# A graph layer with a convolution by points: columns of a bin side by side, and one transpose for the distance factors of m

## The chip, the cores and the metric

The kernel runs on one core of a Trainium2 chip. TensorE multiplies matrices and writes PSUM; VectorE (DVE in the profile), ScalarE (ACT) and GpSimd (POOL) work on elements; SyncE (SP) and POOL issue most of the DMAs. The metric is device time in microseconds from the first to the last instruction of one execution; the median of three executions stands for the kernel. The profiled execution is a further one, with a time of its own.

## What is computed

For 64 graphs of 256 nodes with 256 channels (all float32), after a layer norm and a ReLU that give `h`:

```
xc     = transpose(h)                                      # channels, nodes
c      = relu(bn1(conv1(xc)))                              # 1 tap
x_conv = relu(bn2(conv2(c)) + xc)                          # 17 taps
s      = h @ w_se.T + b_se                                 # 3 numbers a node
dist   = |s_n|^2 + |s_m|^2 - 2 s_n.s_m
A      = exp(-dist) * adj
x_nmp  = A @ relu(h @ w_msg.T + b_msg)
out    = x + GRU([x_conv, x_nmp], h)                       # gates r, z, n
```

The GRU's products are the largest part: 768 inputs and outputs of gates by 256 nodes for each graph, from three sources (`h`, `x_nmp`, `x_conv`).

## The kernel before

**Tiling.** Two graphs (`G`) make an item `i`, a tile of 512 columns; there are 32 items. Four items make a batch `b` of eight graphs (`GB`), and the main loop (line 1000) runs over eight batches. In a batch the second convolution is done for all eight graphs; the other parts are done item by item.

**The second convolution.** It is computed by evaluating polynomials at points. The 256 nodes of a graph are 16 residues by 16 blocks (`NW`). `split_steps(j)` (line 691) takes item j's output `h1` of the first convolution and writes differences to `V` and sums to `U`; `fft.odd` and `fft.even` turn these into 16 bins of (mostly) complex values, with `T`, `Sv` and `PT` as further tiles. `products(b, m)` (line 744) then multiplies, for each bin, three operands by three 256x256 weight matrices, on TensorE: the moving operand of one product is one bin of one half of the channels, 8 graphs by 16 blocks, 128 columns. The results go to `Yv` and `Yu`, and `branch_back`, `odd_back`, `q_back`, `p_back` and `join(j)` lead back to nodes; `join(j)` ends with `residual` for item j (lines 786 to 789: L788 on VectorE, L789 on ScalarE), and gives that item's `x_conv`.

All these tiles are seen through `Slots` (line 28): partition, then graph and half of the channels (16), then real or imaginary, then slot n, then 16 blocks. One bin's columns for one half of the channels so lie in 8 pieces of 16, `v[:, k::DC, 0, :]` at line 757. `Yu` is `V` itself: when the products no longer need `V`, the results are written over it, in the same layout, so that `split_steps(j)` of the next batch overwrites just what `join(j)` has read.

**Distances.** `message(i)` (line 792) computes messages and the three numbers `s`, and fills `Z`: block 0 with factors of n (for each of four chunks of nodes -2s, s^2, 1), and blocks 1 and 2 with factors of m (s, 1, s^2) for the two chunks of m, each repeated for the four rows of chunks. `embed(i)` (line 815) transposes the three blocks and copies them to `ZT` at once. `affinity(i)` (line 822) makes four small products of `ZT` with itself, an exponential of each on ScalarE (L830), and a product with `adj` on VectorE (L836).

**Gates.** `gates(i, dc)` (line 865) starts the products with `h` and `x_nmp`, calls `early` after those of r, calls `wait` before the products with `x_conv`, and ends with tanh on ScalarE (L889 `tr`, L896 `nn`, L905 `tz`) and VectorE's parts (L891 to L913). Its PSUM tiles come from a ring of five, `acc`; another ring of three is `aux`.

**Order.** It is written out by hand: every engine works through its instructions in the order in which the program issues them. For VectorE a planner, `Pace` (line 236), keeps a queue of small steps (splits, transforms, joins, statistics). It estimates TensorE's and VectorE's times while the program is written, and issues steps from the queue where VectorE is expected to be free; `flush(mark)` issues all up to a mark. So the order of `pace.add` is VectorE's order among these steps. The part of the loop that the change touches is in lines 1048 to 1094: after the products, the last backward steps end with the mark `scaled`, then follow `join(0)`, statistics of another item and `join(1)`; in the gates of the batch's first item `wait` flushes `scaled`, issues `affinity(i + 2)` and the first convolution of the next batch's first item (`conv1(nxt)`), queues `split_steps(nxt)`, then `join(2)`. `join(3)` is queued after the second gates and `conv1(nxt + 1)`.

Of the kernel before, what the change touches and what calls it, by code (L numbers as in the profile page):

```python
# [13 lines left out]
FP = mybir.dt.float32  # L14
U16 = mybir.dt.uint16
AF = mybir.ActivationFunctionType
# [11 lines left out]
class Slots:  # L28

    def __init__(self, t, A, n, E):
        self.t = t.rearrange("p (a c n e) -> p a c n e", a=A, c=2, n=n)

    def __call__(self, c, s, n=1, step=1):
        if c is None:
            v = self.t.rearrange("p a c n e -> p (a c) n e")
        else:
            v = self.t[:, :, c]
        return v[:, :, s:s + step * (n - 1) + 1:step, :]  # L40
# [261 lines left out]
def kernel(  # L302
# [26 lines left out]
    nc = tc.nc  # L329
    P = 128  # L330
    B, N, D = x.shape
    G = 2
    GB = 8
    PB = GB // G
    NB = B // GB
    DC = D // P
    MC = N // P
    W = G * N
    TAPS = c2_wT.shape[1]
    SE = se_wT.shape[1]  # L340
    KD = 3 * SE
    Q = 32
    L = 16
    NW = N // L
# [4 lines left out]
    const = ctx.enter_context(tc.tile_pool(name="const", bufs=1))  # L349
# [19 lines left out]
    def chunk(t, g, c):  # L369
        return t[:, g * N + c * P:g * N + (c + 1) * P]  # L370


    X, ADJ, Y = {}, {}, {}
# [62 lines left out]
    Ut, Vt = (const.tile([P, SL], FP, name=n) for n in ("U", "V"))  # L436
    PTt, Svt, Tt = (const.tile([P, SL // 2], FP, name=n) for n in ("PT", "Sv", "T"))
    SPARE = {2: Svt, 3: PTt}
    fft = Fft(nc.vector, nc.scalar)
# [74 lines left out]
    pace = Pace()  # L514

    def mm(p, w, v, columns, **kw):
        nc.tensor.matmul(p, w, v, **kw)  # L517
        pace.tensor(columns)

    def transpose(p, v):  # L520
        nc.tensor.transpose(p, v, ident)  # L521
        pace.tensor(P / 2)

    def aux():
        return psum.tile([P, W], FP, name="aux", bufs=3)

    def acc():
        return psum.tile([P, W], FP, name="acc", bufs=5)
# [76 lines left out]
    s1, h1_shift = fold_bn(bn1, "bn1")  # L605


    Z = const.tile([P, 1 + MC, G * MC, Q], FP, name="z")
    nc.gpsimd.memset(Z, 0.0)
    nc.gpsimd.memset(Z[:, 0, :, 2 * SE:KD], 1.0)  # L610
    nc.gpsimd.memset(Z[:, 1:, :, SE:2 * SE], 1.0)
    ZT = const.tile([P, (1 + MC) * P], FP, name="zT")

    h1 = const.tile([P, G * DC, L, NW + 2], FP, name="h1")
    nc.gpsimd.memset(h1, 0.0)

    U, V = (Slots(t, GB * DC, L // 2, NW) for t in (Ut, Vt))
    PT, Sv, T = (Slots(t, GB * DC, L // 4, NW) for t in (PTt, Svt, Tt))
    Yu = V


    def transpose_h(i):
# [52 lines left out]
    def conv1(i, other=acc):  # L675
        if i >= B // G:
            return
        for o in range(DC):
            p = acc() if o == 0 else other()
            for k in range(DC):  # L680
                mm(p, w_c1[:, k, o * P:(o + 1) * P], HT[i][:, k, :], W, start=(k == 0), stop=(k == DC - 1))
            v = h1.rearrange("p (g o) s b -> p o g s b", o=DC)[:, o, :, :, 1:1 + NW]
            u = p.rearrange("p (g s b) -> p g s b", g=G, b=NW)
            if i == 0:
                nc.vector.tensor_scalar(v, u, s1[:, o:o + 1], h1_shift[:, o:o + 1], ALU.mult, ALU.add)
                nc.vector.tensor_scalar(v, v, 0.0, None, ALU.max)
            else:
                nc.scalar.activation(v, u, AF.Relu, bias=h1_shift[:, o:o + 1], scale=s1[:, o:o + 1])
        pace.vector(0, pace.pe + ACT)

    def split_steps(i):
        if i >= B // G:
            return []
        j = i % PB
        hv = h1.rearrange("p a (c h) b -> p (a c) h b", c=2)
        A = slice(2 * G * j * DC, 2 * G * (j + 1) * DC)
        q = []
        for s, b in ((4, 0), (0, 1)):
            a, bb = hv[:, :, s:s + 4, b:b + NW], hv[:, :, s:s + 4, b + 1:b + 1 + NW]
            q += [fft.sub(V(None, s, 4)[:, A], a, bb), fft.add(U(None, s, 4)[:, A], a, bb)]  # L700
        return q


# [40 lines left out]
    def products(b, m, between=None):  # L744
        p = [acc() for _ in range(3)]
        for n in range(2):
            if n and between:
                between()
            for kind, v in enumerate(operands(2 * m + n)):
                if v is None:  # L750
                    load_kind(b, 2 * m + n + 3, kind)
                    continue
                for o in range(DC):
                    for k in range(DC):
                        mm(p[kind][:, (n * DC + o) * P:(n * DC + o + 1) * P],
                           WB[b, 2 * m + n, kind][:, k, o * P:(o + 1) * P],
                           v[:, k::DC, 0, :], P, start=(k == 0), stop=(k == DC - 1))
                load_kind(b, 2 * m + n + 3, kind)
        p1 = work.tile([P, W], FP, name="p1")
        pv = [t.rearrange("p (n a e) -> p a n e", n=2, e=NW) for t in (p1, p[1], p[2])]  # L760
        if m < 7:
            nc.scalar.copy(p1, p[0])
            if m < 4:
                re, im = Yv(m % 2, m // 2 * 2, 2), Yv(m % 2, 4 + m // 2 * 2, 2)
            elif m < 6:
                re, im = Yu(m - 4, 0, 2), Yu(m - 4, 2, 2)
            else:
                t = Yu.t[:, :, :, 6:8, :].rearrange("p a c n e -> p n a c e")
                re, im = t[:, 0], t[:, 1]
            pace.vector(2 * W, pace.pe + PSUM)  # L770
            nc.vector.tensor_sub(re, pv[0], pv[2])  # L771
            nc.vector.tensor_add(im, pv[0], pv[1])  # L772
        else:
            half = W // 2
            nc.scalar.copy(p1[:, :half], p[0][:, :half])
            nc.scalar.mul(Yu(0, 4)[:, :, 0, :], p[0][:, half:].rearrange("p (a e) -> p a e", e=NW), 0.5)
            nc.scalar.mul(Yu(1, 4)[:, :, 0, :], p[1][:, half:].rearrange("p (a e) -> p a e", e=NW), 0.5)
            pace.vector(W, pace.pe + PSUM)
            nc.vector.tensor_sub(Yu(0, 5)[:, :, 0], pv[0][:, :, 0], pv[2][:, :, 0])
            nc.vector.tensor_add(Yu(1, 5)[:, :, 0], pv[0][:, :, 0], pv[1][:, :, 0])  # L780
# [11 lines left out]
    def message(i):  # L792
        MSG[i] = work.tile([P, G, MC, D + SE], FP, name="msg")
        for g in range(G):
            for c in range(MC):
                p = acc() if g * MC + c == 3 else aux()
                for k in range(DC):
                    mm(p[:, :D + SE], chunk(HT[i][:, k], g, c), w_msg[:, k, :], D + SE,
                       start=(k == 0), stop=(k == DC - 1))
                pace.vector(D, pace.pe + PSUM)  # L800
                nc.vector.tensor_add(MSG[i][:, g, c, :], p[:, :D + SE], b_msg)  # L801
        s = MSG[i][:, :, :, D:]
        flat = s.rearrange("p g c s -> p (g c) s")
        nc.scalar.mul(Z[:, 0, :, :SE], flat, -2.0)
        nc.scalar.activation(Z[:, 0, :, SE:2 * SE], flat, AF.Square)
        for c in range(MC):
            z = Z[:, 1 + c].rearrange("p (g x) s -> p g x s", x=MC)
            for x in range(MC):
                nc.scalar.copy(z[:, :, x, :SE], s[:, :, c])
                nc.scalar.activation(z[:, :, x, 2 * SE:KD], s[:, :, c], AF.Square)  # L810
        for g in range(G):
            nc.scalar.activation(MSG[i][:, g, :, :D], MSG[i][:, g, :, :D], AF.Relu)


    def embed(i):
        p = aux()
        for j in range(1 + MC):
            transpose(p[:, j * P:(j + 1) * P], Z[:, j].rearrange("p q s -> p (q s)"))
        nc.scalar.copy(ZT, p[:, :(1 + MC) * P])


    def affinity(i):
# [116 lines left out]
    odd, even, halved, scaled = (Mark() for _ in range(4))  # L939
# [1 line left out]
    joined = [Mark() for _ in range(PB)]  # L941

    def forward():
        pace.add(fft.odd(V, T, Sv), odd)
        pace.add(fft.even(U, PT, T), even)

    w_ih = const.tile([P, 2 * DC, 3 * D], FP)
    w_hh = const.tile([P, DC, 3 * D], FP)
# [51 lines left out]
    for b in range(NB):  # L1000
        i = b * PB
# [48 lines left out]
        def join(j):  # L1050
            pace.add(fft.join(Yu, Yv, T, slice(2 * G * j, 2 * G * (j + 1))))
            pace.add([(W, lambda o=o: residual(i + j, o)) for o in range(DC)], joined[j])
# [10 lines left out]
        pace.flush(normed[1])  # L1063
        turn_h(nxt + 1)

        def wait():
            pace.flush(scaled)
            affinity(i + 2)
            conv1(nxt, aux)
            pace.add(split_steps(nxt), halved)  # L1070
            join(2)
            pace.flush(joined[0])
        gates(i, 0, wait, lambda i=i: embed(i + 2))
        if b == 0:
            transpose_a(i + 2)
            load_y(0)
# [5 lines left out]
        def early():  # L1082
            join_h(nxt + 1)
            pace.flush(normed[2])
            turn_h(nxt + 2)
        gates(i, 1, None, early)
        pace.flush(halved)
        conv1(nxt + 1)
        join(3)
        pace.add(split_steps(nxt + 1), halved)  # L1090
        pace.add(norm_steps(nxt + 3)[0], normed[3])
        aggregate(i + 2)
# [87 lines left out]
```

## Time and profile before

| | |
|---|---|
| median of three executions | 1830.07 us (1827.06 to 1830.39) |
| profiled execution: time, span | 1830.99 us, 1829.2 us |
| TensorE matmuls | 7494 instructions, busy 98% of the span |
| TensorE weight loads | 7494, 61% |
| VectorE | 2596 instructions, 75% |
| ScalarE | 1444 instructions, 40% |
| GpSimd | 357 instructions, 12% |
| granted TensorE clock | 0.995 |
| HBM | 156.6 MB read, 44.3 MB written, 110 GB/s |

The page gives each engine's busy time, the chain of work that ended last, and groups of instructions (line, engine, operation, output<-inputs, shape, count, then busy time, mean duration in ns, and the engine's idle time before them with what ended it). A timeline row gives a start in us from the span's start, a busy time, and a count of merged instructions. One float32 matmul of the program is two instructions in the trace, and most matmuls stand under L517, the helper that issues them; the vector steps of the convolution stand under L59 to L65, and the scalings under L68, for the same reason. Matmuls overlap in the pipeline, so the distance from one start to the next says more than a duration.

### The profile page before, as it was taken

Reading aid. Unit: us, or ns where it says so; the run is one execution under the profiler, and the core shown is the slowest. Engines: PE = TensorE matmul, PEld = TensorE weight load, DVE = VectorE, ACT = ScalarE, POOL = GpSimd, SP = SyncE. Lnnn points to the kernel's source line nnn. Section 1 sums busy time; section 2 is a strip of 40 time slices with the busy share of each in tenths; the row PEclk is TensorE's granted clock in tenths of the full one; section 3 lists DMA queues with packets and bytes.
Section 4 is the critical chain, followed back from the end, with each engine's and each line's share of the span. In section 5 each row is a group of like instructions: output and inputs, shape, how many; then the busy total and the mean of one; then the engine's idle time right before and its main releaser. Section 6 shows DMA issues by size and latency. Waiting matters only on the chain.

```text
span 1829.2 us, 21881 instructions
## 1 busy us (share of the span) xinstructions
PE 1794.1 (98%) x7494; PEld 1112.1 (61%) x7494; DVE 1367.0 (75%) x2596; ACT 727.6 (40%) x1444; POOL 220.7 (12%) x357
## 2 busy tenths in 40 slices
PE   5999999999999999999999999999999999999998
PEld 3787454964569544784448645595546944487453
DVE  4889669795879849797697967888587984979422
ACT  2525532364323642255422653236432463224321
POOL 2210102101111011111012000110111110111000
PEclk9999999999999999999999999999999999999999
DMA  7777553854538444564347545385544744164011
GB/s 197 242 256 229 114 105 91 244 138 113 108 95 257 104 104 92 156 192 119 85 99 218 163 98 107 87 261 119 115 101 121 222 106 95 41 187 114 8 39 35
DMA packets 250482, 245.96 MB, mean 134 GB/s; under 512 B 142936, under 2 KB 176500, under 8 KB 250371
## 3 DMA queue, kind: packets, MB, share of 16 engines
q1 hardware_dynamic: 216634, 183.83, 36.9%
q0 software_dynamic: 30784, 58.07, 13.9%
q10 hardware_dynamic: 2953, 2.66, 0.7%
q8 instruction: 59, 0.97, 0.2%
q14 instruction: 52, 0.43, 0.1%
HBM read 156.56 MB, written 44.30 MB: 110 GB/s over the span
## 4 chain that ended last, share of the span: by engine, by line
PE 93%; DMA 3%; DVE 2%; ACT 1%; issue 0%; SPq 0%; ACTq 0%; DVEq 0%
PE acc L517 80%; PE aux L517 10%; PE aux L521 2%; DMA taps<-in_c_wT_dram 2%; PE aux L829 1%; DMA filt<-fo 1%; DVE Yv L59 1%; DMA wb<-filt 0%; DVE T L65 0%; DVE Yv L62 0%; DVE msg L801 0%; ACT fo L716 0%; DVE st L559 0%; DVE Yv L771 0%; DVE V L772 0%
## 5 line engine op out<-in xcount | busy, mean ns | idle before, releaser
L517 PE MATMUL acc<-xnm,w_ih 128*128 128x512 f32 x768 | 353.1, 592 | 0.0
L517 PE MATMUL acc<-hT,w_hh 128*128 128x512 f32 x768 | 350.5, 592 | 0.0
L517 PE MATMUL acc<-Yv,w_ih 128*128 128x512 f32 x768 | 342.7, 596 | 1.9 <-ACT Yv L789 1.9
L517 PEld LDWEIGHTS acc<-Yv,w_ih 128*128 128x128 f32 x768 | 145.8, 191 | 185.4 <-issue 182.8
L517 PEld LDWEIGHTS acc<-xnm,w_ih 128*128 128x128 f32 x768 | 144.7, 190 | 176.0 <-issue 174.1
L517 PEld LDWEIGHTS acc<-hT,w_hh 128*128 128x128 f32 x768 | 143.9, 190 | 164.6 <-issue 154.3
L891 DVE SCALAR_TENSOR_TENSOR gn<-tr,gn 128x512 f32<-128x512 f32 x64 | 44.2, 690 | 200.2 <-ACT tr L889 200.1
L889 ACT ACTIVATE tr<-acc,b_rz 128x512 f32<-128x512 f32 x64 | 44.0, 687 | 354.6 <-PE acc L517 354.6
L925 POOL DMA_DIRECT2D out_dram<-y x62 | 38.2, 620 | 789.1 <-DVE y L924 763.9
L517 PE MATMUL acc<-V,wb 128*128 128x128 f32 x1024 | 124.8, 275 | 0.0
L517 PE MATMUL acc<-U,wb 128*128 128x128 f32 x1024 | 124.3, 276 | 0.0
L517 PEld LDWEIGHTS acc<-U,wb 128*128 128x128 f32 x1024 | 120.4, 192 | 3.5 <-DVE T L59 2.0
L59 DVE SCALAR_TENSOR_TENSOR V<-T,V 128x256 f32<-128x256 f32 (+2 forms) x224 | 121.8, 612 | 0.3
L517 PEld LDWEIGHTS acc<-V,wb 128*128 128x128 f32 x1024 | 119.5, 192 | 0.0
L517 PE MATMUL acc<-hT,w_c 128*128 128x512 f32 x228 | 106.5, 608 | 1.7 <-ACT hT L633 1.3
L517 PE MATMUL aux<-e,msg 128*128 128x256 f32 x464 | 104.9, 379 | 0.0
L517 PEld LDWEIGHTS aux<-e,msg 128*128 128x128 f32 x464 | 87.1, 190 | 17.7 <-issue 6.9
L565 POOL TENSOR_TENSOR rstd<-rstd,neg_half 128x4 f32<-128x4 f32 x32 | 38.6, 1207 | 478.1 <-DVE shift L567 425.1
L896 ACT ACTIVATE nn<-gn,bn_columns 128x512 f32<-128x512 f32 x64 | 46.2, 722 | 116.7 <-DVE gn L894 116.7
L517 PE MATMUL aux<-w_msg,hT 128*128 128x259 f32 x384 | 89.5, 382 | 0.0
L517 PEld LDWEIGHTS aux<-w_msg,hT 128*128 128x128 f32 x384 | 72.2, 190 | 17.1 <-issue 7.2
L426 ACT COPY adj<-adjh 128x1024 uint16<-128x1024 uint16 x58 | 74.1, 1345 | 21.0 <-DMA adjh<-halves_d 21.0
(163 smaller groups left out, 2710.8 us busy)
## 6 DMA issues: line engine op xcount, KB each, us to landing
wb<-filt SPq DMA_DIRECT2D x376, 256.0 KB
y<-in_x_dram POOLq DMA_DIRECT2D x64, 256.0 KB, 5.5
out_dram<-y POOLq DMA_DIRECT2D x62, 256.0 KB, 5.7
x<-in_x_dram SPq DMA_DIRECT2D x60, 256.0 KB
halves_d<-halves SPq DMA_DIRECT2D x116, 128.0 KB
adjh<-halves_d POOLq DMA_DIRECT2D x116, 128.0 KB, 5.4
hh<-halves SPq DMA_DIRECT2D x108, 128.0 KB
filt<-fo POOLq DMA_DIRECT2D x18, 252.0 KB, 5.0
```

Source lines behind the costliest of these rows:

```text
L59: return self.step(out, lambda: self.v.scalar_tensor_tensor(out, x, s, y, op0=ALU.mult, op1=ALU.add))
L426: nc.scalar.copy(v[:, j], u[:, j])
L517: nc.tensor.matmul(p, w, v, **kw)
L521: nc.tensor.transpose(p, v, ident)
L565: nc.gpsimd.tensor_tensor(t["rstd"], t["rstd"], neg_half, ALU.pow)
L829: nc.tensor.matmul(p[:, :N], ZT[rows_q, :P], ZT[rows_q, P:], start=True, stop=True)
L889: nc.scalar.activation(tr, pr, AF.Tanh, bias=b_rz[:, dc:dc + 1], scale=0.5)
L891: nc.vector.scalar_tensor_tensor(gn, tr, 1.0, gn, op0=ALU.add, op1=ALU.mult)
L896: nc.scalar.activation(nn, gn, AF.Tanh, bias=b_ih[:, 2 * DC + dc:2 * DC + dc + 1])
L925: eng.dma_start(out=rows(out, G * i + g), in_=row_tile(Y[i], g))
```

## The change

Forward and backward sides get layouts of their own. A new class `Columns` has partition, half of the channels k, real or imaginary, slot n, and then 128 columns (8 graphs by 16 blocks). `U`, `V`, `PT`, `Sv` and the forward view of `T` (`Tx`) use it; `Yu` and the backward `T` keep `Slots`, on the same memory. A product's moving operand is now `v[:, k, 0, :]`. A split writes one graph at a time (eight steps of half the size), and, as item 0's split now overwrites columns of all eight graphs' `Yu`, `join(2)` and `join(3)` are queued ahead of `split_steps(nxt)`.

`Z` loses a block: the factors of m are written and transposed once for all four chunks, and `embed` copies them out in eight pieces of 32 partitions, to the rows where they are needed, after a copy of the factors of n. In the gates of the batch's first item `flush(scaled)` and `embed(i + 2)` now both stand in `early`.

```diff
+class Columns:
+    def __init__(self, t, K, n, X):
+        self.t = t.rearrange("p (k c n x) -> p k c n x", k=K, c=2, n=n)
+
+    def __call__(self, c, s, n=1, step=1):
+        if c is None:
+            v = self.t.rearrange("p k c n x -> p (k c) n x")
+        else:
+            v = self.t[:, :, c]
+        return v[:, :, s:s + step * (n - 1) + 1:step, :]
...
-    Z = const.tile([P, 1 + MC, G * MC, Q], FP, name="z")
+    Z = const.tile([P, 2, G * MC, Q], FP, name="z")
...
-    U, V = (Slots(t, GB * DC, L // 2, NW) for t in (Ut, Vt))
-    PT, Sv, T = (Slots(t, GB * DC, L // 4, NW) for t in (PTt, Svt, Tt))
-    Yu = V
+    U, V = (Columns(t, DC, L // 2, GB * NW) for t in (Ut, Vt))
+    PT, Sv, Tx = (Columns(t, DC, L // 4, GB * NW) for t in (PTt, Svt, Tt))
+    Yu = Slots(Vt, GB * DC, L // 2, NW)
+    T = Slots(Tt, GB * DC, L // 4, NW)
...
-        hv = h1.rearrange("p a (c h) b -> p (a c) h b", c=2)
-        A = slice(2 * G * j * DC, 2 * G * (j + 1) * DC)
         q = []
         for s, b in ((4, 0), (0, 1)):
-            a, bb = hv[:, :, s:s + 4, b:b + NW], hv[:, :, s:s + 4, b + 1:b + 1 + NW]
-            q += [fft.sub(V(None, s, 4)[:, A], a, bb), fft.add(U(None, s, 4)[:, A], a, bb)]
+            for g in range(G):
+                hv = h1[:, g * DC:(g + 1) * DC].rearrange("p a (c h) b -> p (a c) h b", c=2)
+                x = slice((G * j + g) * NW, (G * j + g + 1) * NW)
+                a, bb = hv[:, :, s:s + 4, b:b + NW], hv[:, :, s:s + 4, b + 1:b + 1 + NW]
+                q += [fft.sub(V(None, s, 4)[:, :, :, x], a, bb), fft.add(U(None, s, 4)[:, :, :, x], a, bb)]
...
-                           v[:, k::DC, 0, :], P, start=(k == 0), stop=(k == DC - 1))
+                           v[:, k, 0, :], P, start=(k == 0), stop=(k == DC - 1))
...
-        for c in range(MC):
-            z = Z[:, 1 + c].rearrange("p (g x) s -> p g x s", x=MC)
-            for x in range(MC):
-                nc.scalar.copy(z[:, :, x, :SE], s[:, :, c])
-                nc.scalar.activation(z[:, :, x, 2 * SE:KD], s[:, :, c], AF.Square)
+        nc.scalar.copy(Z[:, 1, :, :SE], flat)
+        nc.scalar.activation(Z[:, 1, :, 2 * SE:KD], flat, AF.Square)
...
-        for j in range(1 + MC):
+        for j in range(2):
             transpose(p[:, j * P:(j + 1) * P], Z[:, j].rearrange("p q s -> p (q s)"))
-        nc.scalar.copy(ZT, p[:, :(1 + MC) * P])
+        nc.scalar.copy(ZT[:, :P], p[:, :P])
+        for q in range(G * MC):
+            for c in range(MC):
+                m = q // MC * MC + c
+                nc.scalar.copy(ZT[q * Q:(q + 1) * Q, (1 + c) * P:(2 + c) * P], p[m * Q:(m + 1) * Q, P:2 * P])
...
-        pace.add(fft.odd(V, T, Sv), odd)
-        pace.add(fft.even(U, PT, T), even)
+        pace.add(fft.odd(V, Tx, Sv), odd)
+        pace.add(fft.even(U, PT, Tx), even)
...
+        def early():
+            pace.flush(scaled)
+            embed(i + 2)
+
         def wait():
-            pace.flush(scaled)
             affinity(i + 2)
             conv1(nxt, aux)
+            join(2)
+            join(3)
             pace.add(split_steps(nxt), halved)
-            join(2)
             pace.flush(joined[0])
-        gates(i, 0, wait, lambda i=i: embed(i + 2))
+        gates(i, 0, wait, early)
...
         conv1(nxt + 1)
-        join(3)
         pace.add(split_steps(nxt + 1), halved)
```

## The prediction

> **What bounds the kernel now.** I read the page's busy shares first, then its chain of work that ended last, then the groups of instructions by shape, then the timelines of TensorE, ScalarE and VectorE over the fourth of the eight batches.
>
> ```profile
> PE 1794.1 (98%) x7494; PEld 1112.1 (61%) x7494; DVE 1367.0 (75%) x2596; ACT 727.6 (40%) x1444; POOL 220.7 (12%) x357
> PE 93%; DMA 3%; DVE 2%; ACT 1%; issue 0%; SPq 0%; ACTq 0%; DVEq 0%
> ```
>
> The chain is TensorE for 93% of the span. Its first products of a batch start at 105.8, 322.7, 538.4, 754.0 and 969.7 us, so a batch takes 215.6 us, and the view of waits names from 106 us on only two waiters on TensorE, for 2.9 us (the last transposes) and 1.9 us (1687 us). A TensorE instruction that gets shorter after 106 us shortens the end by as much, as long as no new wait appears.
>
> ```profile
> L517 PE MATMUL acc<-V,wb 128*128 128x128 f32 x1024 | 124.8, 275 | 0.0
> L517 PE MATMUL acc<-U,wb 128*128 128x128 f32 x1024 | 124.3, 276 | 0.0
> L517 PE MATMUL acc<-Sv,wb 128*128 128x128 f32 x512 | 68.4, 277 | 0.0
> L517 PE MATMUL acc<-PT,wb 128*128 128x128 f32 x448 | 55.3, 275 | 0.0
> L521 PE MATMUL aux<-ident,d 128*128 128x128 f32 x256 | 33.6, 273 | 2.9 <-DVE d L913 2.9
> ```
>
> These are the products of the second convolution, 1024+1024+512+448 = 3008 instructions of 128 columns, and a transpose of the same width. A mean duration overlaps the next instruction, so I take distances between starts:
>
> ```profile
> 734.19 1.04 PE L521 MATMUL aux<-ident,d 128*128 128x128 f32 x8
> 735.07 3.60 PE L517 MATMUL acc<-hT,w_hh 128*128 128x512 f32 x8
> 738.50 3.60 PE L517 MATMUL acc<-xnm,w_ih 128*128 128x512 f32 x8
> ...
> 777.50 3.62 PE L517 MATMUL aux<-e,msg 128*128 128x256 f32 x16
> 780.96 5.52 PE L517 MATMUL acc<-U,wb 128*128 128x128 f32 x48
> 786.32 2.80 PE L517 MATMUL aux<-w_msg,hT 128*128 128x259 f32 x12
> ```
>
> 48 products take 786.32 - 780.96 = 5.36 us, 111.7 ns each (the starts themselves give 111.65 for all four groups). 512 columns take 3.43 / 8 = 429 ns (429.2), 256 columns 3.46 / 16 = 216 ns (215.9). A line through these two is 0.833 ns a column plus 2.6 ns, hence 109.3 ns at 128 columns, and the transposes do take 109.1. The products are 2.5 ns over that line. They alone read their moving operand in eight pieces of 16 columns.
>
> **What the skill says.** "TensorE: Matmul & The Clock Gate", section "Wait — 56ns, not 53.3ns?", has a fixed 2.5 ns beside a time by columns; the line above agrees (2.6). Its section "Back-to-back issue gap" says that a stream of weight load and matmul pairs is paced by both, so the weight load could be the 2.5 ns. The trace speaks against it: a product is 111 or 112 ns from the next start also where a transpose follows, with its shorter weight load (140 ns recorded, against 192), and a transpose is 109 ns before a product, though the product's 192 ns weight load runs beneath it. The excess goes with the matmul that reads pieces. "SBUF — State Buffer", section "Door 1: The DMA port swizzle", says that a read keeps full rate if it takes more than one element from each 16-byte line, four fp32; pieces of 64 bytes would then cost nothing, and the 2.5 ns have no explanation there. This is the main doubt. The page "Advanced Engine Details and Errata", section "Engine Queue Depths", gives ScalarE and VectorE a queue of 8; the trace shows them working in program order, which matters below.
>
> **The change, part by part.**
>
> *Products in one piece.* 3008 x (111.65 - 109.15) = 7.5 us less on TensorE, all after 105.8 us. No trace shows this read in one piece; the bounds are 0 (pieces are not the cause) and 7.5. I take 7.5.
>
> *One transpose of Z fewer.* 32 x 0.109 us; the first batch's first one lies in the filter stage, where TensorE waits anyway, so 31 x 0.109 = 3.4 us.
>
> *Six small ScalarE instructions fewer per message* (two of 12 elements for eight of 6). From 816.34 to 817.12 us eight take 0.78 us; two take about 0.20. That is 0.58 us earlier for all behind them. Once a batch, in batches two to eight (792.6, 1008.2 us and so on), the transposes of z wait for these: 0.20 to 0.28 us between two transposes and 0.055 after them, 0.26 x 7 = 1.8 us, which goes.
>
> *Nine copies to zT for one.* The 128x384 copy holds ScalarE 0.36 us (820.70 to 821.05). The trace has no copy of 32x128. Small copies hold it 0.085 us for 6 elements, an exponential of 256 elements out of PSUM 0.264, so 128 elements hold it 0.085 + 122 x 0.000716 = 0.17 us and nine 1.56: 1.2 us more. Bounds: 0.085 each (0.4 more) and 0.36 each (2.9 more). Affinity, the next reader, starts on TensorE 5.3 to 5.8 us after the z transposes in three of four places of a batch, and 2.9 us after in the second (copies would end at about 794.9, affinity starts at 795.9). These hide it. In the filter stage the copy starts at 96.1 and delays affinity to about 97.8, but TensorE's next work waits until 98.65 for a ScalarE copy that waits for a write to DRAM: hidden. The place to fear is the third:
>
> ```profile
> 820.13 0.67 ACT L878 ACTIVATE gn<-acc,bn_columns 128x512 f32<-128x512 f32 x1
> 820.70 0.46 ACT L819 COPY zT<-aux 128x384 f32<-128x384 f32 x1
> 821.05 0.63 ACT L68 ACTIVATE Yv<-Yv 128x512 f32<-128x512 f32 x1
> 821.58 1.66 ACT L68 ACTIVATE V<-V 128x512 f32<-128x512 f32 x3
> 824.86 0.94 ACT L830 ACTIVATE e<-aux 128x256 f32<-128x256 f32 x3 [1.62 <-PE acc L829]
> ```
>
> Here the change also puts the four L68 scalings ahead of the zT copies. New order: gn at 820.13 - 0.58 = 819.55, scalings 820.1 to 822.2, nine copies 822.2 to 823.75, the last landing 0.27 after its start, at 823.85. Affinity stood at 824.13, now 824.02. Margin 0.17 us; no wait.
>
> *Joins 2 and 3 before the first split.* VectorE's join(0) waits for the last scaling, so it starts at 822.34, not 823.28:
>
> ```profile
> 823.28 0.69 DVE L62 TENSOR_TENSOR T<-V 128x512 f32<-128x512 f32 x1 [2.23 <-ACT V L68]
> ...
> 833.87 1.41 DVE L788 SCALAR_TENSOR_TENSOR Yv<-Yv,bn_scale,hT 128x512 f32<-128x512 f32 x2
> ```
>
> From there, by the same rows: join 3.98, statistics 1.95, two steps of join(1) 1.33, the four mask products 2.0, two steps 1.32: L788 of join(1) at 832.9. In the new ScalarE order one L789 of join(1) stands ahead of the gate's L889, which so goes from 830.2 to about 834.3 and frees its PSUM buffer at 835.0. TensorE wants that buffer for the next gate's r product at 835.07: margin 0. The next, pn's buffer, is freed by L894 at about 838.2 and wanted at 838.5. Join(2), the second gate's parts and join(3) then end at about 845.5 and the split, 8 x 0.335 = 2.7 us, at 848.2; ScalarE's next write of h1 comes at 850.8. The two L789 of join(2) now stand ahead of the second gate's L878 and the copies and scalings behind it, so the transposing DMA of h on SP's queue goes from 844.4 to about 845.8; its result is read by the first convolution at 871. No queue of SP or POOL has its DMAs in another order. So no stall by the sum, with three margins near zero. I charge 0.1 us a batch, 0.8 in all; the lower bound is 0, the upper 2 us a batch.
>
> *Splits in two.* Eight 128x256 instead of four 128x512: 8 x 0.335 against 4 x 0.60, 0.3 us x 32 = 9 us more VectorE. The four at the start are hidden, since Sv is ready at 87.4 and read at 105.8; later forward transforms end at 717.0 for a read at 754.0. The other steps keep their element counts, and at 512 elements VectorE takes 0.69 us in pieces (V<-T) as in one run (gn): nothing.
>
> *Last batch.* TensorE waits there 2.0 us at 1687 us for an L789 that stands behind the exponentials on ScalarE, in the new order too, and then runs four matmuls at half pace (1.6 us more). Unchanged.
>
> **Sum.** -7.5 - 3.4 - 1.8 + 0.8 = -11.9 us. Against the profiled execution, 1830.99 us (span 1829.2), that is 1819.1; against the median of 1830.07 us it is **1818.2 us**.
>
> **Rivals.** (A) *The pieces are not what costs 2.5 ns*, or only half of it: then -4.4 to -8 us, 1822 to 1825.7. For it: the SBUF page. Against: the 109 and 111.7 ns at each handover. (B) *The third affinity becomes a wait, and the kernel slower.* At the upper price the copies run from 822.2 to 825.4 and land 0.1 later, 1.5 us after affinity's 824.02. At 1687 us a wait of 2.0 us was followed by 1.6 us of half pace. 1.5 + 1.6 = 3.1 us x 8 = 25, less 12.7: +12, 1842 us. It decides from (12.7 / 8) = 1.6 us a batch, half pace included. Against: the copy is as small as those that take 0.085. (C) *VectorE's longer run before the split stalls the gates by PSUM*: 0.5 to 1 us a batch, 4 to 8 us, 1822 to 1826. For it: the margin of 0. Against: join(0) starts 0.9 us earlier.
>
> **How the numbers follow.** The main case has 0.66, its own range 1816 to 1821.5. A has 0.12, C 0.09, B 0.09, and 0.04 is left for what I don't see. About 0.2% (3.7 us) is what three runs between 1827.06 and 1830.39 us can tell from no change. The range 1815.5 to 1826 holds the main case and most of A and C. Main case, A, C, B and the rest, in that order, give faster: 0.66 + 0.11 + 0.05 + 0.00 + 0.01 = 0.83; same: 0.00 + 0.01 + 0.02 + 0.02 + 0.01 = 0.06; slower: 0.02 + 0.07 + 0.02 = 0.11, from the last three.
>
> **What would show it.** Starts of products 109 ns apart, 48 in 5.24 us; transposes of z in twos; a batch of 215.6 - 1.5 = 214.1 us; no wait of TensorE on zT, and none of tens of ns on the r product's buffer; L889 some 4 us later in the first gates. Products still at 111.7 ns make A right; TensorE waiting on zT near the third affinity, with half pace after it, makes B right.

## The result, and the profile after

The changed kernel takes 1829.69 us (median of four executions, 1827.75 to 1831.1) against 1830.15 us for the kernel before (four executions). The ratio, estimated from all the runs and not from the two medians, is 1.0001 with a 95% interval of 0.9983 to 1.0018: no change, where 1818.2 us was forecast. The profiled execution took 1828.58 us with a span of 1826.8 us, 2.4 us less than that of before.

The page of the changed kernel, its busy shares, its chain and the groups of the products (a line number of before is some 15 to 20 higher now: the products are L532, the transposes L536):

```profile
PE 1793.7 (98%) x7462; PEld 1111.0 (61%) x7462; DVE 1373.6 (75%) x2724; ACT 763.2 (42%) x1508; POOL 218.1 (12%) x357
PE 95%; issue 2%; DMA 1%; POOL 1%; DVE 0%; ACT 0%; ACTq 0%; POOLq 0%
L532 PE MATMUL acc<-V,wb 128*128 128x128 f32 x1024 | 124.8, 275 | 0.0
L532 PE MATMUL acc<-U,wb 128*128 128x128 f32 x1024 | 124.2, 276 | 0.0
```

32 transposes are gone (7462 instructions for 7494), and ScalarE and VectorE have the added work. But TensorE's busy time fell by 0.4 us only, and the two groups of products have, within 0.1 us, the busy time and the mean duration that they had. The same stretch of the fourth batch on TensorE's timeline (start in us, busy time, count of merged instructions):

```profile
775.89 3.62 PE L532 MATMUL aux<-e,msg 128*128 128x256 f32 x16
779.34 5.52 PE L532 MATMUL acc<-U,wb 128*128 128x128 f32 x48
784.70 2.80 PE L532 MATMUL aux<-w_msg,hT 128*128 128x259 f32 x12
790.89 0.38 PE L536 MATMUL aux<-ident,z 128*128 128x128 f32 x2
```

48 products take 784.70 - 779.34 = 5.36 us, as before: 111.7 ns each, though each now reads its 128 columns in one piece. The largest term of the forecast is zero. The transposes of z do come in twos.

Where the rest went is seen at the third affinity of the batch. On TensorE, first in the kernel before, where it is 824.77 - 824.13 = 0.64 us from the first of the four small products to the next matmul (in between, rows are left out):

```profile
824.13 0.49 PE L829 MATMUL aux<-zT 9*128 9x256 f32 x3
...
824.77 1.98 PE L517 MATMUL acc<-hT,w_c 128*128 128x512 f32 x4
```

Then in the changed kernel, TensorE and ScalarE:

```profile
822.13 1.00 PE L849 MATMUL aux<-zT 9*128 9x256 f32 x5
822.65 0.48 PE L849 MATMUL acc<-zT 9*128 9x256 f32 x1
822.97 0.37 PE L849 MATMUL aux<-zT 9*128 9x256 f32 x1
822.97 0.37 PE L849 MATMUL acc<-zT 9*128 9x256 f32 x1
823.28 1.98 PE L532 MATMUL acc<-hT,w_c 128*128 128x512 f32 x4
```

```profile
815.68 2.07 ACT L665 ACTIVATE hh<-x,shift,rstd 128x256 f32<-128x256 f32 x4
817.65 0.68 ACT L898 ACTIVATE gn<-acc,bn_columns 128x512 f32<-128x512 f32 x1
818.22 0.63 ACT L83 ACTIVATE Yv<-Yv 128x512 f32<-128x512 f32 x1
818.74 1.67 ACT L83 ACTIVATE V<-V 128x512 f32<-128x512 f32 x3
820.30 0.26 ACT L835 COPY zT<-aux 128x128 f32<-128x128 f32 x1
820.44 2.15 ACT L839 COPY zT<-aux 32x128 f32<-32x128 f32 x8
822.86 0.94 ACT L850 ACTIVATE e<-aux 128x256 f32<-128x256 f32 x3 [0.27 <-PE aux L849]
```

The scalings (L83) run ahead of the copies to `zT`, as the change puts them. The eight copies of 32 partitions start at 820.44, 820.71, 820.99, 821.25, 821.53, 821.80, 822.07 and 822.34 us: 0.27 us from one to the next. The last has landed at 822.59, while affinity began at 822.13. When all of `zT` is there, the four products of an affinity run over each other, and it takes 0.644 us from its first start to the next matmul's; here two of them begin some 0.5 us late, and it takes 823.28 - 822.13 = 1.15 us. The view of waits, after 104 us, first of the kernel before, then of the changed one (what waited, for what, us in all, times, the longest):

```profile
PEld aux L521 <- ACT z L810: 1.8, 7, 0.3
```

```profile
PEld aux L849 <- ACT zT L839: 7.0, 14, 0.8
```

The old wait, of the weight loads of z's transposes for the small ScalarE instructions, is gone. A new one, of affinity's weight loads for the last copies, comes 14 times.

By distances between starts a batch became shorter by 0.436 us (four transposes) and 0.262 us (the old wait), and longer by 0.51 us at the third affinity and 0.10 us at the second: 0.09 us less, 215.63 to 215.54 us. Of the 2.4 us by which the spans differ, 1.6 us lie before the first product (105.78 to 104.19 us), a stage that took 103.1 to 106.3 us in the profiles of all kernels of the layer here; the eight batches together hold 0.8 us.

### The profile page after: what moved, and what is told of

Read it like the earlier page. It is cut to its first block, busy times and chain, and to the rows that moved or that the text cites. A ratio compares the mean times of both kernels' runs of the same rounds, so it can differ in the third digit from the quotient of the medians.

```text
span 1826.8 us, 22058 instructions
## 1 busy us (share of the span) xinstructions
PE 1793.7 (98%) x7462; PEld 1111.0 (61%) x7462; DVE 1373.6 (75%) x2724; ACT 763.2 (42%) x1508; POOL 218.1 (12%) x357
## 4 chain that ended last, share of the span: by engine, by line
PE 95%; issue 2%; DMA 1%; POOL 1%; DVE 0%; ACT 0%; ACTq 0%; POOLq 0%
PE acc L532 80%; PE aux L532 11%; PE aux L536 2%; PE aux L849 1%; DMA taps<-in_c_wT_dram 1%; POOL filt L735 0%; DMA filt<-fo 0%; DMA points<-points 0%; POOL rstd L580 0%; ACT zT L839 0%; DVE y L944 0%; DVE Sv L586 0%; DVE V L80 0%; DVE U L77 0%; DVE st L574 0%
## 5 line engine op out<-in xcount | busy, mean ns | idle before, releaser
L532 PE MATMUL acc<-xnm,w_ih 128*128 128x512 f32 x768 | 353.1, 592 | 0.0
L532 PE MATMUL acc<-hT,w_hh 128*128 128x512 f32 x768 | 350.5, 592 | 0.0
L532 PE MATMUL acc<-Yv,w_ih 128*128 128x512 f32 x768 | 342.7, 596 | 1.9 <-ACT Yv L807 1.9
L532 PEld LDWEIGHTS acc<-Yv,w_ih 128*128 128x128 f32 x768 | 145.7, 191 | 185.4 <-issue 181.2
L532 PEld LDWEIGHTS acc<-xnm,w_ih 128*128 128x128 f32 x768 | 144.7, 190 | 176.0 <-issue 175.6
L532 PEld LDWEIGHTS acc<-hT,w_hh 128*128 128x128 f32 x768 | 143.9, 190 | 164.6 <-issue 154.0
L909 ACT ACTIVATE tr<-acc,b_rz 128x512 f32<-128x512 f32 x64 | 43.8, 685 | 337.7 <-PE acc L532 337.2
L532 PE MATMUL acc<-V,wb 128*128 128x128 f32 x1024 | 124.8, 275 | 0.0
L532 PE MATMUL acc<-U,wb 128*128 128x128 f32 x1024 | 124.2, 276 | 0.0
L532 PEld LDWEIGHTS acc<-U,wb 128*128 128x128 f32 x1024 | 120.0, 192 | 3.6 <-DVE T L74 2.0
L532 PEld LDWEIGHTS acc<-V,wb 128*128 128x128 f32 x1024 | 119.5, 192 | 0.0
L532 PE MATMUL acc<-hT,w_c 128*128 128x512 f32 x228 | 106.9, 610 | 1.3 <-ACT hT L650 1.3
L532 PE MATMUL aux<-e,msg 128*128 128x256 f32 x464 | 104.9, 379 | 0.0
L532 PEld LDWEIGHTS aux<-e,msg 128*128 128x128 f32 x464 | 87.1, 190 | 17.7 <-issue 5.7
L532 PE MATMUL aux<-w_msg,hT 128*128 128x259 f32 x384 | 89.4, 382 | 0.0
L532 PEld LDWEIGHTS aux<-w_msg,hT 128*128 128x128 f32 x384 | 72.2, 190 | 17.2 <-issue 7.2
```

The source lines that it names most:

```text
L909: nc.scalar.activation(tr, pr, AF.Tanh, bias=b_rz[:, dc:dc + 1], scale=0.5)
```

## The experiments

Two questions: what paces the products, and where the gains from the z part went. For the first, *pieces* is the forecast's theory, and *load* its rival: a product of 128 columns cannot start before the next 128x128 weights are loaded, however its data lie.

**A kernel of matmuls and copies alone.** It computes nothing of the layer. Each variant issues 24 float32 matmuls (48 instructions in the trace) after a warm-up, and then there are small copies on ScalarE. In short form, a few of the variants:

```diff
+    nc.tensor.matmul(acc[j % 6][:128, :128], w[:, 128 * (j % 4):128 * (j % 4) + 128], v[:, :, 16 * (j % 4):16 * (j % 4) + 16], ...)    # L68
+    nc.tensor.matmul(acc[j % 6][:128, :128], w[:, 128 * (j % 4):128 * (j % 4) + 128], flat[:, 128 * (j % 4):128 * (j % 4) + 128], ...) # L71
+    nc.tensor.matmul(acc[j % 6][:64, :128], w[:, 128 * (j % 4):128 * (j % 4) + 64], v[:, :, 16 * (j % 4):16 * (j % 4) + 16], ...)      # L74
...
+    nc.scalar.copy(dst[:32, 128 * j:128 * j + 128], src[:32, 128 * (j % 4):128 * (j % 4) + 128])               # L102
+    q = 32 * (j % 4)
+    nc.scalar.copy(dst[q:q + 32, 128 * j:128 * j + 128], src[q:q + 32, 128 * (j % 4):128 * (j % 4) + 128])     # L105
```

> A kernel of its own, which computes nothing of the layer: streams of 24 float32 products each (48 instructions) after a warm stream, and series of 12 ScalarE copies. If a product is paced by its own weight load (load theory), the distance of starts is about 111.65 ns with 128 weight columns and 128 moving columns, in pieces of 16 and in one piece alike, stays about 111.65 with 96 moving columns, and is 109.2 with 64 or 112 weight columns, in pieces and in one; 132 and 160 moving columns give 112.5 and 135.8. If the read in pieces costs it (the prediction's theory), 128 weight columns give 111.65 in pieces and 109.2 in one, 64 weight columns the same two values, and 96 moving columns 82.5. Copies: if copies of 32 partitions on ScalarE don't overlap when the partitions change from one to the next, those that stay are about 0.145 us apart and those that move on about 0.27; if every 32-partition copy is slow, all are 0.27; if it is the crossing to other partitions, only those that cross.

TensorE's timeline of this kernel (the shape before "f32" is the weights' rows*columns, then the moving operand):

```profile
47.40 5.52 PE L68 MATMUL acc<-v,w 128*128 128x128 f32 x48
52.75 5.52 PE L71 MATMUL acc<-v,w 128*128 128x128 f32 x48
58.21 5.45 PE L74 MATMUL acc<-v,w 128*64 128x128 f32 x48
63.50 5.40 PE L77 MATMUL acc<-v,w 128*64 128x128 f32 x48
```

Distances between starts, from the same trace (each the mean of a series without its first):

```
weights 128 columns, moving 8 pieces of 16    111.67 ns
weights 128 columns, moving one run of 128    111.67
weights  64 columns, moving 8 pieces of 16    109.15
weights  64 columns, moving one run of 128    109.15
weights 112 columns, moving one run of 128    109.17
weights 128 columns, moving one run of 96     111.65
weights 128 columns, moving one run of 132    112.50
weights 128 columns, moving one run of 160    135.83
weights  64 columns, moving 32 pieces of 4    109.15
weights  64 columns, moving 128 single elements, 32 bytes apart    232.00
```

This rules out *pieces*: pieces of 16, and even of 4, cost nothing. What sets the pace goes with the number of weight columns, as *load* has it. With 128 weight columns an instruction takes 111.65 ns even if it moves only 96 columns; with 132 moving columns it takes 112.50, what the prediction's line by columns gives (132 x 0.833 + 2.6 = 112.6). With 112 or 64 weight columns the 128 moving columns set the pace, at 109.2. (Fewer weight columns also mean fewer rows of the result. That it is the load and not these rows is seen at the first matmul of L68, whose weights were loaded beneath a matmul of 512 columns: it writes 128 rows too, and takes 109 ns to the next start. So does the first product after a wider matmul in the layer; see the part on the prediction.) The Trainium skill had both halves right: "TensorE: Matmul & The Clock Gate", section "Back-to-back issue gap", on pairs paced by both, and "SBUF — State Buffer", section "Door 1: The DMA port swizzle", on pieces that are free while more than one element of a 16-byte line is used (109.15 ns here in pieces of four, and 232.00 for single elements; pieces of two were not run).

The copies, on ScalarE's timeline of the same kernel:

```profile
108.94 2.02 ACT L102 COPY dst<-src 32x128 f32<-32x128 f32 x12
110.82 3.38 ACT L105 COPY dst<-src 32x128 f32<-32x128 f32 x12
114.22 3.33 ACT L108 COPY dst<-src 32x128 f32<-32x128 f32 x12
117.56 2.01 ACT L110 COPY dst<-src 32x128 f32<-32x128 f32 x12
```

L102 stays on partitions 0 to 31, L105 goes on by 32 partitions each time (input and output alike), L108 does so with the output on other partitions than the input, L110 reads always 0 to 31 and writes always 32 to 63. 12 copies take 1.88 us where the partitions stay, 3.40 us where they move: 0.157 us and 0.280 us each. The forecast's 0.17 us is near the price of copies that stay; those of the change move.

**Half of the weights' columns in the layer itself.** In the kernel before, the second product of each sum (k = 1) uses 64 of its 128 weight columns, and the two are not summed. Half of that product's rows and the sum are left out.

```diff
-                        mm(p[kind][:, (n * DC + o) * P:(n * DC + o + 1) * P],
-                           WB[b, 2 * m + n, kind][:, k, o * P:(o + 1) * P],
-                           v[:, k::DC, 0, :], P, start=(k == 0), stop=(k == DC - 1))
+                        w = P // 2 if k else P
+                        mm(p[kind][:w, (n * DC + o) * P:(n * DC + o + 1) * P],
+                           WB[b, 2 * m + n, kind][:, k, o * P:o * P + w],
+                           v[:, k::DC, 0, :], P, start=True, stop=True)
```

> The kernel before, in pieces, with the second half of the contraction (k = 1) of each product of the second convolution using 64 instead of 128 weight columns, and no sum over the two halves; so half of its values are left out. Load theory: of the four instructions of a pair the two that follow a short load are 2.5 ns shorter, mean 110.4 instead of 111.65, a batch 0.47 us shorter (215.16 instead of 215.63). Read theory: 111.65 throughout, a batch of 215.63.

It took 2074.26 us, beside 1827.59 us for one run of the kernel before: both theories missed. From TensorE's timeline (rows of both widths are merged here, under the shape of the first):

```profile
105.25 3.19 PE L517 MATMUL acc<-V,wb 128*128 128x128 f32 x16
108.37 1.63 PE L517 MATMUL acc<-Sv,wb 128*128 128x128 f32 x8
```

16 products take 108.37 - 105.25 = 3.12 us; their starts lie 213, 205, 160 and 202 ns apart, in turn, a mean of 195. So 3008 x (195 - 111.65) = 251 us, where 247 were measured. Changing between 128 and 64 weight columns at every second instruction makes every instruction slow, so that it no longer compares loads of two widths. The run says nothing on the pieces; it asks for a run of its own, below.

**The layout alone.** The change's `Columns`, split by graphs and order of joins, with the old `Z`, `embed` and place of `flush(scaled)`.

```diff
 (to the changed kernel)
-        for j in range(2):
+        for j in range(1 + MC):
...
-        def early():
-            pace.flush(scaled)
-            embed(i + 2)
         def wait():
+            pace.flush(scaled)
             affinity(i + 2)
...
-        gates(i, 0, wait, early)
+        gates(i, 0, wait, lambda i=i: embed(i + 2))
```

> The change's layout and join order alone, with Z, embed and the place of the flush as before. Load theory: products 111.65 ns apart, batch 215.63 us as before, less than 0.1 us either way. Read theory: 109.15 ns and 214.7 us a batch.

1828.82 us beside 1827.59, one run each. Single times can't tell so small a difference (37 runs of the kernel before, below, lie between 1824.85 and 1832.61 us); the trace can. From TensorE's timeline:

```profile
778.80 5.52 PE L532 MATMUL acc<-U,wb 128*128 128x128 f32 x48
784.15 2.14 PE L532 MATMUL aux<-w_msg,hT 128*128 128x259 f32 x9
```

Products at 5.35 / 48 = 111.5 ns (111.65 by starts), every affinity 0.644 us, a batch 215.63 us, to the hundredth what it was. The layout, the splits in two and the new order of joins gain nothing and lose nothing.

**The z part alone.** The new `Z` and `embed` in the kernel before, with `flush(scaled)` left after `embed(i + 2)`.

```diff
 (to the kernel before)
-    Z = const.tile([P, 1 + MC, G * MC, Q], FP, name="z")
+    Z = const.tile([P, 2, G * MC, Q], FP, name="z")
...
-        nc.scalar.copy(ZT, p[:, :(1 + MC) * P])
+        nc.scalar.copy(ZT[:, :P], p[:, :P])
+        for q in range(G * MC):
+            for c in range(MC):
+                m = q // MC * MC + c
+                nc.scalar.copy(ZT[q * Q:(q + 1) * Q, (1 + c) * P:(2 + c) * P], p[m * Q:(m + 1) * Q, P:2 * P])
```

> The change's Z and embed alone, with the layout, the joins and the place of the flush as before. The transposes and the wait for z give -0.70 us a batch. If the third affinity is late in the kernel after because the scalings go first, it isn't late here: a batch of 215.63 - 0.70 + 0.10 = 215.03 us, unless the scalings, now behind nine copies, let VectorE's first join start so late that TensorE waits for its result (up to 0.5 us, at the first product with the convolution's output). If the layout paid for something, the result differs.

1830.32 us beside 1827.59; a batch takes 215.87 us, 0.24 more than before. ScalarE's, VectorE's and TensorE's timelines there:

```profile
818.19 2.15 ACT L820 COPY zT<-aux 32x128 f32<-32x128 f32 x8
820.37 0.63 ACT L68 ACTIVATE Yv<-Yv 128x512 f32<-128x512 f32 x1
820.90 1.65 ACT L68 ACTIVATE V<-V 128x512 f32<-128x512 f32 x3
```

```profile
822.59 0.69 DVE L62 TENSOR_TENSOR T<-V 128x512 f32<-128x512 f32 x1 [3.61 <-ACT V L68]
```

```profile
822.59 1.98 PE L517 MATMUL acc<-hT,w_c 128*128 128x512 f32 x4
824.41 1.88 PE L517 MATMUL aux<-hT,w_c 128*128 128x512 f32 x4
826.86 5.42 PE L517 MATMUL acc<-Yv,w_ih 128*128 128x512 f32 x12 [0.57 <-ACT Yv L789]
```

With the copies first, the third affinity is whole again (0.644 us). But now the scalings come late, VectorE's first join starts with them (it waited 3.61 us), and TensorE waits 0.57 us for the `x_conv` that the join makes: from `aux<-hT,w_c` to `acc<-Yv,w_ih` it is 826.86 - 824.41 = 2.45 us, where the kernel before has 828.31 - 826.60 = 1.71, so 0.74 us more. The first matmul after the wait then takes 533 ns to the next start instead of 429, another 0.10. With 0.09 at the second affinity, that turns the gain of 0.70 us into the loss of 0.24. The nine copies hold ScalarE from 818.05 to 820.37, 2.3 us in place of 0.36. So in either order ScalarE's added time, about 2 us, reaches TensorE: through affinity if the copies come last, through the join if they come first. Moving `flush(scaled)` ahead, as the change does, is the better of the two (0.61 us against 0.74 + 0.10 + 0.09).

**The changed kernel, with four other ScalarE instructions out of the way.** On ScalarE's timeline of the changed kernel, four L665 instructions (`hh`, 2 us) stand ahead of gn, the scalings and the copies. They are `turn_h(nxt + 1)`, the norm of an item whose transposed `h` is wanted much later. This run issues them behind `embed(i + 2)`; nothing else differs.

```diff
-        turn_h(nxt + 1)
         def early():
             pace.flush(scaled)
             embed(i + 2)
+            turn_h(nxt + 1)
```

> The kernel after, with the four hh scalings of the next batch (2.0 us of ScalarE) moved from ahead of the first gate to behind the nine zT copies. If the nine copies, 0.27 us each, are what splits the third affinity, they end about 2 us earlier and affinity is whole again: TensorE 0.64 us on it instead of 1.15, a batch of 215.04 us instead of 215.55, the kernel about 4.2 us under the kernel before (0.23%, hardly clear of noise). If what splits it is something else, the batch stays at 215.55.

1824.91 us (median of 18 runs) against 1830.4 for the kernel before (37 runs): ratio 0.9973, interval 0.9966 to 0.9981. That is 0.27% less, a small difference but clear of the noise. The changed kernel was not timed beside it; its four executions took 1827.75 to 1831.1 us. ScalarE's timeline, then TensorE's:

```profile
815.61 0.67 ACT L898 ACTIVATE gn<-acc,bn_columns 128x512 f32<-128x512 f32 x1
818.40 2.16 ACT L839 COPY zT<-aux 32x128 f32<-32x128 f32 x8
820.58 2.08 ACT L665 ACTIVATE hh<-x,shift,rstd 128x256 f32<-128x256 f32 x4
822.77 0.94 ACT L850 ACTIVATE e<-aux 128x256 f32<-128x256 f32 x3
```

```profile
822.04 0.49 PE L849 MATMUL aux<-zT 9*128 9x256 f32 x3
822.06 0.48 PE L849 MATMUL acc<-zT 9*128 9x256 f32 x1
822.36 0.39 PE L849 MATMUL aux<-zT 9*128 9x256 f32 x3
822.38 0.37 PE L849 MATMUL acc<-zT 9*128 9x256 f32 x1
822.68 1.99 PE L532 MATMUL acc<-hT,w_c 128*128 128x512 f32 x4
```

The copies end at 820.6, the four affinity products run over each other, 0.644 us in all, and the batch takes 215.03 us, 0.51 less than in the changed kernel: just what the third affinity had lost. And 215.63 - 0.70 + 0.10 (still lost at the second affinity) is 215.03, so the move itself adds nothing. This shows the cause: the change's own gains were real, and the late copies ate most of them.

**The same move with the z part alone** (the run of the z part above, with `turn_h(nxt + 1)` put behind `flush(scaled)`, ahead of `affinity(i + 2)`).

```diff
-        turn_h(nxt + 1)
         def wait():
             pace.flush(scaled)
+            turn_h(nxt + 1)
             affinity(i + 2)
```

> The change's Z and embed alone in the kernel before, with the hh scalings moved behind the nine copies and the scalings of the backward transform. The copies and those scalings end before VectorE needs them, and the wait of 0.74 us at the convolution's output goes: a batch of 215.63 - 0.70 + 0.09 = 215.03 us, as in the run beside it, so that the layout makes no difference. If the layout helps or harms by itself, the two differ.

1826.65 us (21 runs), ratio 0.9985, interval 0.9978 to 0.9991. A batch takes 215.03 to 215.10 us, as with the layout, so that the layout is worth nothing per batch here either. What separates it from the run before is the end of the last batch. TensorE's timelines there, of this run and of the run before it:

```profile
1686.23 7.11 PE L517 MATMUL acc<-Yv,w_ih 128*128 128x512 f32 x12 [2.56 <-ACT Yv L789]
```

```profile
1684.90 5.42 PE L532 MATMUL acc<-Yv,w_ih 128*128 128x512 f32 x12 [1.89 <-ACT Yv L807]
```

This run waits longer, and the twelve matmuls after the wait take 7.11 us in place of 5.42: TensorE's granted clock was one half for 3.41 us after the wait here, and full in the run before.

The record of the granted clock lets us look closer. In every trace of this case it changes only at whole multiples of 3.41 us from its first entry, and that entry lies elsewhere in each execution (18.43 to 25.11 us in the layer's traces). In the six traces of the layer with half pace after this wait, the kernel before and the changed one among them, the whole wait, 1.88 or about 2.57 us, lies within one such period. In the run before this one it lies across two, 0.38 and 1.50 us, and no half pace follows. So the 1.7 us that its profile saves there may be luck of that execution. (This fits seven traces at one place of the program; no run moved a wait against the periods. In the filter stage idle time alone doesn't sort the cases: half pace followed a period with 0.54 us idle in one trace and not one with 1.22 us in another.)

For all the executions the mean granted clock is on record: 0.9952 over 18 runs of the run before, 0.9947 over 21 of this one, 0.9950 over 37 of the kernel before. The difference of these two runs is worth about 1.0 us by an estimate (0.00055 x 1826 us), and with the wait longer by 0.68 us that is about the 1.74 us between their medians. Against the kernel before the clock explains only some 0.4 us of the 5.5, by the same estimate.

**Changing widths, and which side of a copy moves.** A second kernel of matmuls and copies alone; matmuls of 128 weight columns alternate with narrower ones.

```diff
+    nc.tensor.matmul(..., w[:, 128 * (j % 4):128 * (j % 4) + (64 if j % 2 else 128)], flat[:, 128 * (j % 4):128 * (j % 4) + 128], ...)   # L71; 96 at L77
...
+    nc.scalar.copy(dst[q:q + 32, 128 * j:128 * j + 128], src[:32, 128 * (j % 4):128 * (j % 4) + 128])    # only the output moves
+    nc.scalar.copy(dst[:32, 128 * j:128 * j + 128], src[q:q + 32, 128 * (j % 4):128 * (j % 4) + 128])    # only the input moves
```

> Streams of products and copies alone, nothing of the layer. Products with 64, 96, 112 or 120 weight columns in turn with 128: if a weight load is hidden only behind a matmul of the same number of 32-column groups, 64 and 96 in turn with 128 give a mean of about 195 ns as in the run with half weights (205, 160, 202, 213), while 112 and 120, which use all four groups, stay at 109 to 112; if any change of width costs, all four are slow. 96 alone: 109.2. Copies of 32 partitions: moving input alone, moving output alone, moving every third, 128 partitions from SBUF; if only a move of the output's (or only of the input's) start costs, one of the first two is at 0.157 us and the other at 0.28.

```profile
47.77 5.52 PE L68 MATMUL acc<-v,w 128*128 128x128 f32 x48
53.13 9.34 PE L71 MATMUL acc<-v,w 128*128 128x128 f32 x48
62.30 5.40 PE L74 MATMUL acc<-v,w 128*64 128x128 f32 x48
67.64 5.57 PE L77 MATMUL acc<-v,w 128*128 128x128 f32 x48
```

128 and 64 in turn (L71) take 195 ns an instruction, with the layer's 205, 160, 202 and 214 in turn. But 128 and 96 in turn (L77) take 110.4, and so do 112 and 120, so the expectation that 96 would be as slow as 64, by groups of 32 columns, was wrong. Of the widths tried only 64 made a change slow: against 128, and in the first kernel also against 112 (203 and 200 ns around one change). Why is open. Where 128 alternates with 96, 112 or 120, the distances are 109, 109, 112, 112: each instruction pays for its own weights. A copy of 32x128 takes 0.272 us if only its output moves and 0.271 us if only its input does; where one in three moves, that one alone takes 0.28.

## Why the prediction was wrong, by its own steps

*Products in one piece*, -7.5 us: **zero**. This step failed, and with it 63% of the sum: the read in pieces costs nothing, and the 2.5 ns go with the load of 128 weight columns. The bounds, 0 to 7.5, were right, and so was the doubt named there; the choice of 7.5 rested on the handover between products and transposes. That reading was off by one instruction. By the distances, what a matmul pays for its own weights lies between its recorded start and the *next* start, not ahead of its own. The trace of before had the answer. The first product after a matmul of 256 or 259 columns, whose own weights were loaded beneath that long matmul, is 108 to 110 ns from the next in all 23 places, reading eight pieces like all others; every later one is 111 or 112 from its next. The durations say it too. This is one line's view of the kernel before, from 780.8 to 781.8 us (durations as least, median and greatest):

```profile
L517 PE MATMUL acc<-U,wb x8: 272/275/275, 781.0 to 781.7; 128*128 128x128 f32 x8
```

One of the eight, the first, lasts 272 ns, and the others 275. The transpose that was "109 ns before a product" was 109 because its own load had been short; the product after it paid for its own. Rival A had the pieces as harmless, at 0.12; that alone would have given 1825.7 us.

*One transpose of Z fewer*, -3.4 us, and *six small ScalarE instructions fewer*, -1.8 us: right, at 0.436 and 0.262 us a batch.

*Nine copies to zT*: the second step that failed. The place was right ("the place to fear is the third") and the price wrong. 0.17 us a copy came from instructions that stay on their partitions; those that move take 0.27. Eight times 0.1 us turned the forecast margin of 0.17 us before the last landing into a lag of 0.46 us after affinity's start, and cost 0.51 us. The second affinity, where the copies were to end 1.0 us ahead (794.9 against 795.9), lost 0.10 us: they end at 793.94, and it begins at 793.88. Together that is 0.61 us a batch and, by the distances of all affinities, 4.5 us in all (the first batch lost only at the third, the last only at the second), in place of 0.8 for every margin. The bound of 0.36 held the true price, and rival B the mechanism; its size, 3.1 us a batch with half pace, was too large, since half of affinity went ahead and no half pace followed.

*Joins before the split*: right. L909 (the old L889), due at about 834.3 in the time of before, ran at 832.45 (this kernel is 1.5 us ahead there, so 833.95), with its buffer free at 833.12 and wanted at 833.68, so that the feared margin of 0 (rival C) was 0.56 us and cost nothing. *Splits in two* and *last batch* were right: 0.335 us a step of a split, and the same 1.9 us of wait at the end.

Put together with what was measured: -3.4 - 1.8 + 4.5 = -0.7 us, and the trace after the first product has -0.8. What came was rival A together with a small rival B, a pair for which the forecast had no number.

## What to carry to other kernels

To tell what paces a stream of matmuls, look at one whose own weight load was certainly hidden (the first after a wider one): if it is short and the rest are not, the load is the limit, and no layout of the moving operand helps. Before one wide copy is split into copies to several partitions, price them at their full latency (0.256 us each here), not at their spacing on one set of partitions (0.157), and look at what they push back in both orders. When a gain vanishes, look for work ahead of the late instruction on its engine that nobody waits for: moving four such ScalarE instructions brought most of the gain back, and made this the fastest of the kernels here.

## What the runs showed of the hardware that was not expected

- 128 weight columns in float32 hold a stream of matmuls at 111.65 ns an instruction, even at 96 moving columns; up to 120 weight columns do not (109.2 at 128 moving columns; 120 was seen in turn with 128 only).
- Matmuls of 128 and of 64 weight columns in turn take 195 ns; 128 with 96, 112 or 120 take 110.4.
- ScalarE copies of 32x128 out of PSUM follow each other at 0.157 us on the same partitions and at 0.27 to 0.28 us if the input's or the output's partitions change from one to the next. VectorE's take 0.198 us and, with both moving, 0.30 us.
- After the same wait of 1.88 us at the last batch, half pace followed in the profiles of the kernel before and of the changed one, and not in that of the changed kernel with `turn_h` moved. There the wait lay across two of the periods of 3.41 us in which the granted clock changes; in the other two it lay within one. A general rule is not shown.
